# A graph layer on one core: the product of x made during the scatters and added by VectorE, and a written order for the last four node tiles

## The chip, the cores and the metric

The kernel runs on one core of a Trainium2 chip. A core has five engines with a queue of instructions each: TensorE (PE, whose weight loads the profile lists apart as PEld), VectorE (DVE), ScalarE (ACT), GpSimd (POOL) and SyncE (SP), and DMA engines that move data between memory and the core's two on-chip stores, SBUF and PSUM (where PE's products land). The engines run side by side and wait for each other by semaphores. The metric is the device time of one execution in microseconds (us).

## The reference

There are 6250 nodes with 128 features (x) and 206,250 edges with 128 features and a node number each (src). With the helper code left out, what is computed is

```python
def _L0_gnn_ref(x, edge_index, edge_features, global_feat, W_c, b_c, W1, b1, W2, b2, W3, b3):
    n = x.shape[0]
    row = edge_index[0]
    edge_aggr = jnp.zeros((n, HIDDEN), dtype=x.dtype).at[row].add(edge_features)
    global_expand = jnp.repeat(global_feat, n // global_feat.shape[0], axis=0)
    combined = jnp.concatenate([x, edge_aggr, global_expand], axis=-1) @ W_c + b_c
    h = jax.nn.softplus(combined @ W1 + b1)
    h = jax.nn.softplus(h @ W2 + b2)
    return h @ W3 + b3

edge_index = jnp.stack([src, dst])
x = _layernorm(x + _L0_gnn_ref(x, edge_index, edge_attr_128, ...), axis=-1)
```

The edges' rows are summed by node; then each node goes through a linear layer on (x, sum, global), two softplus layers, a last linear layer, the residual and a layer norm. All in float32.

## The kernel before, in words

**Sums by node.** The nodes are cut into buckets of 196 nodes (`BL`), and the kernel first brings the edges' rows into memory by bucket (`rows_by`), then sums each bucket with products of one-hot matrices. The edges are taken in columns of 122; two columns are a pair, three pairs a piece, and the pieces belong to eight groups (`GROUPS`). A piece passes through these steps:

- `load_rows`: SP loads 16 columns of edge rows (`rows`); `code_rows`: ACT writes their node numbers behind the features (`rows<-pair_i`, L1112).
- `compare`: a one-hot matrix of the rows' slots (`sort_hot`), by DVE (L1138) and ACT (L1145, L1147) in turn. `gather`: PE multiplies it with the rows (L1158) into one of three PSUM banks (`sorted`). `settle`: ACT copies the bank into one of six sets `pairs` (L1170).
- `scatter_row`: POOL sends a pair to its place in `rows_by` by an indirect DMA (L1187), 846 of them.
- position steps: for the groups ahead, short steps of PE and DVE find each edge's slot (`past` L723, `pair_ib` L494, products L553/L555/L738 into two PSUM banks that the profile calls `small`, `slot` L572).
- For each bucket, `chunks<-rows_by`: SP loads the sorted rows back; DVE makes the one-hot matrix `hot` (L986); PE sums (`part`, L1009); DVE adds the part to the columns of `sums_t` (L1030, L1032), which holds the sums turned (features on partitions, nodes in columns).

**What sets the order.** All of this is issued by hand. Each step is put on a list with a time of a plan in us (`when(t, step)`, `over(steps, t0, t1)` for several evenly apart), the list is sorted, and PE, DVE, ACT and SP issue in this order; POOL follows its own. In the plan a scatter takes 1.3 (`SCATTER`), and a piece's load, coding, compare, gather and settle are placed 36, 21, 17.5, 14 and 10.5 ahead of its first scatter. The profile's times lie near the plan's at first and some 20 us behind them in group 3. SP's queue is in order: a load that waits for its buffer holds all behind it.

**Weights.** `weights()`, planned at 100.0, loads the weights and `x_t`, x turned (128 partitions, 6250 columns; four DMAs). `combine` and `biases` of `node_rows()` work out the folded weights: `fold[:, 0]` = W_c's x part times W1, `fold[:, 1]` = its part for the sums times W1, and the biases; they run in group 3 (`NODES = (3, 4)`), from 477.9 us in the profile.

**The node layers** (`node_layers`, the tail). There are 13 tiles: eleven of 512 nodes, then 248 and 370. Their parts for the layer norm are tiles 0-2, 3-5, 6-8, then "two" (9 and 10, called a and b) and the end (11 and 12, c and d). The loop runs three tiles at once, one in each layer:

- `z_of(1)`: x's product and the sums' product go into one `sorted` bank (L1350, L1351). `decay` and `log1p`: ACT's Abs, Exp, Ln (L1361, L1362, L1367) from the bank to `away`. `softplus`: DVE makes `h` from the bank and `away` (L1375).
- `z_of(2)`: PE's product with W2 (L1354), then the same again. `last_product`: four products with W3 into a `small` bank (L1389).
- `last_layer`: DVE adds x (L1397) and takes mean and variance (L1400, L1404). `norm` (once for a part): DVE, ACT's two roots (L1415, L1416) and DVE again make 1/deviation (`rs`, L1414 to L1419); then y is scaled block by block, by POOL (L1431), in the two last parts every other block by ACT (L1428), at the very end by DVE instead of POOL; and stored.
- `summed_to`: PE's and DVE's sums of the last buckets (L1009, L1032) stand between these steps, as far as the next tile needs them.

The lines that set what `z_of` reads and where `norm` stands:

```python
                nc.tensor.matmul(z[:, :w], fold[:, 0, :], x_t[:, n0:n0 + w], start=True, stop=False)
                nc.tensor.matmul(z[:, :w], fold[:, 1, :], sums_t[:, n0:n0 + w],
                                 start=False, stop=True)
```

## Time and profile before

| what | us |
|---|---|
| median of three runs | 1322.09 (1319.48, 1322.09, 1325.66) |
| the profiled execution | 1324.44 |
| its span | 1322.7 |
| busy in the span: PE, DVE, ACT, POOL | 1170.2, 1073.0, 1064.5, 878.1 |
| POOL's scatters (846, L1187) | 825.7 busy, 329.9 idle before them |
| from 1188 to the end (the last buckets' sums and all node tiles) | 134.7 |

A row of the timeline is: start in us, duration, engine, line, operation, output and inputs with their sizes, xcount for several in a row; in brackets the idle time of the engine just before and what ended it ("DVE slot L572" is the operation on DVE of line 572 that wrote `slot`). A row of the waits is: who waited, for whom, the sum of the waits, how many, and the longest. In a row by line, the numbers behind a colon are the shortest, mean and longest duration in ns and the first and last start. Matmuls are shown by start and duration as a pipeline, so that two that follow each other may overlap.

### The profile page before, as it was taken

To read this page: it belongs to the slowest core of one execution; us is meant where nothing else is said; L and a number is where in the kernel's file an instruction comes from. 1 tells how busy PE (TensorE), PEld (TensorE's weight loads), DVE (VectorE), ACT (ScalarE), POOL (GpSimd) and SP (SyncE) were. 2 spreads that over 40 slices of the span, in tenths; PEclk is the share of its full clock that TensorE was granted. 3 is DMA by queue.
4 is the path that set the end of the run, shared out by engine and by line. 5 is a ranking of instruction groups with operands and counts; after the bars stand their busy time and mean duration, and the time that the engine had idled before them with its cause. 6 is when DMAs were issued, how large, how long until landed. Compare 5 with 4: busy or idle time off the path is not lost.

```text
span 1322.7 us, 26940 instructions
## 1 busy us (share of the span) xinstructions
PE 1170.2 (88%) x8617; PEld 1106.4 (84%) x8617; DVE 1073.0 (81%) x2403; ACT 1064.5 (80%) x2484; POOL 878.1 (66%) x915
## 2 busy tenths in 40 slices
...
GB/s 217 240 279 328 320 327 319 289 321 357 342 343 316 339 349 338 281 304 234 328 289 300 316 329 322 315 300 275 321 332 322 340 330 320 296 248 148 139 86 52
DMA packets 227251, 381.95 MB, mean 289 GB/s; under 512 B 28988, under 2 KB 140292, under 8 KB 226720
## 3 DMA queue, kind: packets, MB, share of 16 engines
...
q8 instruction: 72, 1.18, 0.4%
...
HBM read 237.21 MB, written 147.41 MB: 291 GB/s over the span
## 4 chain that ended last, share of the span: by engine, by line
PE 32%; DMA 28%; DVE 13%; ACT 9%; POOL 8%; issue 8%; SPq 1%; ACTq 0%; DVEq 0%; POOLq 0%
PE part L1009 19%; DMA chunks<-rows_by 11%; DMA rows_by<-pairs,pair 10%; PE sorted L1158 9%; POOL rows_by L1187 8%; DMA rows<-in_edge 6%; ACT pairs L1170 5%; DVE hot L986 3%; ACT sort_hot L1145 2%; DVE past L723 1%; DMA rows_by<-fill 1%; DVE sort_hot L1138 1%; DVE pair_ib L494 1%; DVE slot L572 1%; DVE sums_t L1032 1%
## 5 line engine op out<-in xcount | busy, mean ns | idle before, releaser
L1187 POOL DMA_INDIRECT rows_by<-pairs,pair x846 | 825.7, 976 | 329.9 <-issue 201.1
L1009 PE MATMUL part<-hot,chunks 128*128 128x196 f32 x3516 | 671.7, 334 | 16.9 <-DVE sums_t L1032 11.1
L1170 ACT COPY pairs<-sorted 64x387 f32<-64x387 f32 (+2 forms) x1144 | 542.6, 474 | 80.1 <-PE sorted L1158 60.1
L1009 PEld LDWEIGHTS part<-hot,chunks 128*128 128x128 f32 x3516 | 578.4, 192 | 26.2 <-DVE sums_t L1032 12.5
L1158 PE MATMUL sorted<-rows,sort_hot 122*128 122x129 f32 x3384 | 498.1, 287 | 58.7 <-ACT pairs L1170 49.5
L1158 PEld LDWEIGHTS sorted<-rows,sort_hot 122*128 122x128 f32 x3384 | 454.2, 198 | 72.4 <-ACT pairs L1170 69.6
L986 DVE TENSOR_TENSOR hot<-chunks,both_ps 128x784 f32<-128x784 f32 (+3 forms) x541 | 427.3, 808 | 19.2 <-DMA chunks<-rows_by 18.8
L1145 ACT ACTIVATE sort_hot<-plain,slot 122x128 f32<-122x128 f32 x846 | 278.3, 391 | 11.2 <-DVE slot L572 5.3
L1032 DVE TENSOR_TENSOR sums_t<-sums_t,part 128x392 f32<-128x392 f32 (+1 forms) x262 | 143.1, 546 | 133.7 <-PE part L1009 132.1
L1147 ACT ACTIVATE sort_hot<-sort_hot,ones 122x384 f32<-122x384 f32 (+2 forms) x286 | 174.6, 611 | 9.3
L1138 DVE TENSOR_TENSOR sort_hot<-slot,both_ps 122x384 f32<-122x384 f32 (+2 forms) x286 | 153.9, 539 | 3.2 <-PE sorted L1158 3.0
L494 DVE TENSOR_TENSOR pair_ib<-pair_block,both_ps 122x512 bf16<-122x512 bf16 (+2 forms) x157 | 103.2, 662 | 0.3
L1431 POOL TENSOR_SCALAR y<-y,mv,rs 128x128 f32<-128x128 f32 x40 | 31.1, 785 | 100.1 <-issue 70.8
L572 DVE TENSOR_REDUCE slot<-small 122x16 f32<-122x512 f32 (+2 forms) x109 | 72.6, 666 | 12.9 <-PE small L555 12.7
L1361 ACT ACTIVATE away<-sorted,z_bias 128x512 f32<-128x512 f32 (+2 forms) x13 | 8.5, 656 | 69.2 <-DMA chunks<-rows_by 44.6
L553 PE MATMUL small<-pair_ib,half 122*122 122x512 bf16 (+2 forms) x109 | 43.0, 395 | 14.1 <-DVE slot L572 13.8
L1112 ACT COPY rows<-pair_i 122x16 f32<-122x16 f32 x106 | 22.6, 213 | 37.5 <-DMA rows<-in_edge 36.6
L738 PEld LDWEIGHTS <-past 128*128 128x128 f16 x424 | 24.7, 98 | 20.3 <-DVE past L723 14.7
L738 PE MATMUL small<-jump,past 128*128 128x56 f16 (+3 forms) x424 | 29.1, 189 | 13.5 <-DVE past L723 8.9
L723 DVE TENSOR_TENSOR past<-both_ps,starts 128x512 f16<-128x512 f32 (+1 forms) x61 | 39.7, 663 | 0.2
L555 PEld LDWEIGHTS <-starts_h 128*122 128x122 bf16 x236 | 25.3, 148 | 16.3 <-issue 11.9
L723 DVE TENSOR_TENSOR past<-both_ps,starts_late 128x512 f16<-128x512 f32 (+2 forms) x49 | 32.2, 659 | 0.0
...
## 6 DMA issues: line engine op xcount, KB each, us to landing
...
rows_by<-pairs,pair POOLq DMA_INDIRECT x846
...
```

Source lines behind the costliest of these rows:

```text
L494: nc.vector.tensor_tensor(ib, pair_block[:, cols].unsqueeze(2).to_broadcast([PN, n, SB]), iota_ps[:PN, :SB].unsqueeze(1).to_broadcast([PN, ...
L572: nc.vector.tensor_reduce(to, of, axis=mybir.AxisListType.X, op=ALU.max)
L723: nc.vector.tensor_tensor(past[:, :, a:b], twice_ps[:KB].unsqueeze(1).unsqueeze(1).to_broadcast([KB, 2, b - a, P // 2]), own["starts"][:, ...
L986: nc.vector.tensor_tensor(hot[:, q - a:q - a + m], chunks[j][:, lo:hi + 1:step, D:W].to_broadcast([P, m, BL]), iota_ps.unsqueeze(1).to_bro ...
L1009: nc.tensor.matmul(part[:, b - base_of[v], :], t[:, place_in(j, q), :D], hot[:, q - a], start=first, stop=last)
L1032: nc.vector.tensor_add(here, here, of)
L1138: nc.vector.tensor_tensor(hot[:PN, :m], slot[:PN, at:at + 2 * m - 1:2].unsqueeze(2).to_broadcast([PN, m, P]), slot_ps[:PN].unsqueeze(1).to ...
L1145: nc.scalar.activation(hot[:PN, j], by_slot[:PN], AF.Abs, bias=slot[:PN, at:at + 1], scale=-1.0)
L1147: nc.scalar.activation(hot[:PN, :m], hot[:PN, :m], AF.Relu, bias=ones[:PN, :1], scale=-1.0)
L1158: nc.tensor.matmul(out[:, j, :], hot[:PN, j], rows_at[col // LOAD_COLS][:PN, col % LOAD_COLS, :], start=True, stop=True)
L1170: nc.scalar.copy(sets_at[i][64 * n:64 * n + 64, lo:lo + m, h, :W], out[64 * h:64 * h + 64, :m, :])
L1187: s = nc.gpsimd.indirect_dma_start(out=dst, out_offset=bass.IndirectOffsetOnAxis(ap=at, axis=0), in_=rows[:, j].rearrange("p a b -> p (a b ...
```

## The change

- `weights()` is planned at 60.0 instead of 100.0.
- `combine` and `biases` are planned at 130 and 141 instead of in group 3; `NODES` goes.
- 13 new steps `times` (every 13 from 150): PE multiplies 512 columns of `x_t` with `fold[:, 0]` into a `small` bank; 3.5 of plan later `kept` copies the bank by ACT over the same columns of `x_t`. From then on `x_t` holds the product.
- In the tail `z_of(1)` makes the sums' product alone; `with_x` on DVE adds `x_t` to it into a new SBUF tile `z_x` (three buffers), which ACT and the softplus of layer 1 read in the bank's place. It stands behind the first three steps of `summed_to`, ahead of the remaining ones.
- `norm` is split into `roots` (DVE's first step and ACT's two) and the rest.
- The loop ends four steps earlier, and the layers of tiles a, b, c, d stand in an order written out.

```diff
@@ -64,11 +64,12 @@
 FIRST = 24.0
 SOON, FLAGGED = 4.0, 15.9
 SHARE = 2
+KEPT = 3.5
 PREP, LAG = 0.85, 11.0
 TOGETHER, BEHIND = 2, 1
-AT_END, FIRST_STEPS = 4, 9
+AT_END, FIRST_STEPS, X_STEPS = 4, 9, 3
 MATCHED, MULTIPLIED, RATE = 9.0, 1.5, 0.58
-NODES = (3, 4)
+FOLDED, TIMES, EVERY = 130.0, 150.0, 13.0
 TURNED = 2048
 APART = 3
 BATCH = 4
@@ -1092,7 +1093,16 @@
                 nc.tensor.matmul(small[:, 0, :], b2_all, w_sb["w3"], start=True, stop=True)
                 nc.vector.tensor_add(b3_all, small[:, 0, :], of_weights["b3"])
 
-            return [combine, biases]
+            of = {}
+
+            def times(a, b):
+                of[a] = small_bank().rearrange("p b n -> p (b n)")[:, :b - a]
+                nc.tensor.matmul(of[a], fold[:, 0, :], x_t[:, a:b], start=True, stop=True)
+
+            def kept(a, b):
+                nc.scalar.activation(x_t[:, a:b], of.pop(a), AF.Copy)
+
+            return combine, biases, times, kept
 
         pieces = [(g, t, min(PAIRS, s1 - t)) for g, (s0, s1) in enumerate(groups)
                   for t in range(s0, s1, PAIRS)]
@@ -1275,7 +1285,14 @@
             positions_0 = positions(0)[0]
             over([lambda: node_codes(0), tables] + positions_0[:12] + [more_tables] + positions_0[12:], -8.0, FIRST - 19.0)
             when(FLAGGED, lambda: flags_0[0]())
-            when(100.0, weights)
+            when(60.0, weights)
+            combine, biases, times, kept = node_rows()
+            when(FOLDED, combine)
+            when(FOLDED + LAG, biases)
+            for k, a in enumerate(range(0, N, 4 * P)):
+                t, b = TIMES + k * EVERY, min(N, a + 4 * P)
+                when(t, lambda a=a, b=b: times(a, b))
+                when(t + KEPT, lambda a=a, b=b: kept(a, b))
 
             def fills_left():
                 assert not fills
@@ -1290,7 +1307,6 @@
 
             when(begins[last_pair], count_over)
             when(ends[-1], lambda: fills_left())
-            nodes, held = node_rows(), 0
             ahead_of = {g: [(g + 1, 0)] for g in range(G - 1)}
             ahead_of[GAP - 1] = [(GAP, 1)]
             for k in range(GAP, G):
@@ -1308,15 +1324,7 @@
                         prep += [lambda k=k: node_codes(k)]
                         position_steps[k] = positions(k)
                     prep += position_steps[k][part]
-                if NODES[0] <= g < NODES[1]:
-                    upto = len(nodes)
-                    part = nodes[held:upto]
-                    held = upto
-                    middle = t0 + PREP * (t1 - t0)
-                    over(part, middle, t1)
-                    over(prep, t0, middle)
-                else:
-                    over(prep, t0 if g else 16.0, t0 + PREP * (t1 - t0))
+                over(prep, t0 if g else 16.0, t0 + PREP * (t1 - t0))
             todo = fill_rows()
             done_by = FIRST + SCATTER * todo[-1][0] - SLACK
             for n, (due, _, step) in enumerate(todo):
@@ -1347,12 +1355,15 @@
         def z_of(layer, n0, w):
             z = bank()
             if layer == 1:
-                nc.tensor.matmul(z[:, :w], fold[:, 0, :], x_t[:, n0:n0 + w], start=True, stop=False)
-                nc.tensor.matmul(z[:, :w], fold[:, 1, :], sums_t[:, n0:n0 + w],
-                                 start=False, stop=True)
+                nc.tensor.matmul(z[:, :w], fold[:, 1, :], sums_t[:, n0:n0 + w], start=True, stop=True)
             else:
                 nc.tensor.matmul(z[:, :w], w_sb["w2"], h1.pop(n0)[:, :w], start=True, stop=True)
             sub_z[layer, n0] = [z]
+
+        def with_x(n0, w):
+            z = work.tile([P, 4 * P], F32, name="z_x", bufs=3)
+            nc.vector.tensor_add(z[:, :w], sub_z[1, n0][0][:, :w], x_t[:, n0:n0 + w])
+            sub_z[1, n0] = [z]
 
         def decay(layer, n0, w):
 
@@ -1365,6 +1376,10 @@
         def log1p(layer, n0, w):
             away = sub_z[layer, n0][1]
             nc.scalar.activation(away[:, :w], away[:, :w], AF.Ln, bias=ones[:, :1])
+
+        def away_of(layer, n0, w):
+            decay(layer, n0, w)
+            log1p(layer, n0, w)
 
         def softplus(layer, n0, w):
 
@@ -1405,19 +1420,22 @@
             now["done"].append((n0, w, y, at))
             now["at"] += -(-w // P)
 
-        def norm(now, late, last):
-
+        def roots(now, late, last):
             mv, nb = now["mv"], now["at"]
             rs = work.tile([P, 3, 16], F32, name="rs", bufs=2)
             v, g, t = (rs[:, k, :nb] for k in range(3))
-            minus = work.tile([P, 16], F32, name="minus", bufs=2)[:, :nb]
+            now["roots"] = v, g, t
             nc.vector.tensor_scalar(v, mv[:, :nb, 1], EPS, None, op0=ALU.add)
             nc.scalar.activation(t, v, AF.Ln)
             nc.scalar.activation(g, t, AF.Exp, scale=-0.5)
+
+        def norm(now, late, last):
+            mv, nb, (v, g, t) = now["mv"], now["at"], now["roots"]
             nc.vector.tensor_mul(t, g, g)
             nc.vector.scalar_tensor_tensor(t, t, -0.5, v, op0=ALU.mult, op1=ALU.mult)
             nc.vector.scalar_tensor_tensor(g, t, 1.5, g, op0=ALU.add, op1=ALU.mult)
             if late:
+                minus = work.tile([P, 16], F32, name="minus", bufs=2)[:, :nb]
                 nc.vector.scalar_tensor_tensor(minus, mv[:, :nb, 0], -1.0, g,
                                                op0=ALU.mult, op1=ALU.mult)
             for n0, w, y, at in now["done"]:
@@ -1453,11 +1471,13 @@
             summed_to(0)
             z_of(1, *tiles[0])
             normed = None
-            for step in range(len(tiles) + 2):
-                first, second, third = (tiles[k] if 0 <= k < len(tiles) else None
-                                        for k in (step, step - 1, step - 2))
+            for step in range(len(tiles) - 2):
+                first, second, third = (tiles[k] if k >= 0 else None for k in (step, step - 1, step - 2))
+                summed_to(step + 1, X_STEPS)
+                if first:
+                    with_x(*first)
                 if step + 1 < len(tiles):
-                    summed_to(step + 1, FIRST_STEPS)
+                    summed_to(step + 1, FIRST_STEPS - X_STEPS)
                 if second:
                     z_of(2, *second)
                 if third:
@@ -1467,21 +1487,55 @@
                     last_product(*third)
                 for layer, tile_ in ((1, first), (2, second)):
                     if tile_:
-                        decay(layer, *tile_)
-                        log1p(layer, *tile_)
+                        away_of(layer, *tile_)
                 if third:
                     last_layer(now, *third)
                     if third == parts[k][-1]:
-                        normed = (now, k >= len(parts) - 2, k == len(parts) - 1)
-                if step + 1 < len(tiles):
-                    summed_to(step + 1)
-                    z_of(1, *tiles[step + 1])
+                        normed = (now, False, False)
+                summed_to(step + 1)
+                z_of(1, *tiles[step + 1])
                 for layer, tile_ in ((1, first), (2, second)):
                     if tile_:
                         softplus(layer, *tile_)
-                if normed:
+                if normed and step < len(tiles) - 3:
+                    roots(*normed)
                     norm(*normed)
                     normed = None
+
+            a, b, c, d = tiles[-4:]
+            assert [list(part) for part in parts[-2:]] == [[a, b], [c, d]] and normed
+            two, end = (open_part(part) for part in parts[-2:])
+            with_x(*c)
+            summed_to(len(tiles) - 1)
+            z_of(2, *b)
+            last_product(*a)
+            z_of(1, *d)
+            away_of(1, *c)
+            away_of(2, *b)
+            roots(*normed)
+            last_layer(two, *a)
+            norm(*normed)
+            softplus(1, *c)
+            softplus(2, *b)
+            z_of(2, *c)
+            last_product(*b)
+            with_x(*d)
+            away_of(1, *d)
+            away_of(2, *c)
+            softplus(1, *d)
+            z_of(2, *d)
+            last_layer(two, *b)
+            softplus(2, *c)
+            away_of(2, *d)
+            last_product(*c)
+            softplus(2, *d)
+            roots(two, True, False)
+            last_layer(end, *c)
+            norm(two, True, False)
+            last_product(*d)
+            last_layer(end, *d)
+            roots(end, True, True)
+            norm(end, True, True)
 
     node_layers(rest, lambda: summed["to"])
     slow = ctx.enter_context(tc.tile_pool(name="slow", bufs=1))
```

How the instructions stand now (names with `rows`, `fill`, `chunks` as above; `h_...` with `neg_z` is layer 1, with `neg_b` layer 2).

SP's queue, around the loads of the weights and `x_t`, before:

```order
L291 DMA rows<-in_edge 10x4x516
L291 DMA chunks<-rows_by 128x2x136 x6
L291 DMA rows_by<-fill 128x4x272
L291 DMA weights_sb<-in_weights 128x900
L291 DMA x_t<-in_x_turned 128x2048 x3
L291 DMA x_t<-in_x_turned 128x106
L291 DMA rows<-in_edge 112x4x516
L291 DMA rows<-in_edge 10x4x516
L291 DMA chunks<-rows_by 128x2x136 x2
```

And now:

```order
L292 DMA rows<-in_edge 10x4x516
L292 DMA rows_by<-fill 128x4x272
L292 DMA weights_sb<-in_weights 128x900
L292 DMA x_t<-in_x_turned 128x2048 x3
L292 DMA x_t<-in_x_turned 128x106
L292 DMA rows<-in_edge 112x4x516
L292 DMA rows<-in_edge 10x4x516
L292 DMA rows_by<-fill 128x4x272
```

The five loads stand four rows loads, four fills and the first six chunk loads earlier, and no longer just ahead of the two chunk loads.

ACT's queue among the scatters, where the first copy stands now (nothing stood there before):

```order
L1180 COPY pairs_108<-sorted 64x3x129 x4
L1103 ACTIVATE x_t<-small 128x512
L1155 ACTIVATE sort_hot<-plain,slot 122x128 x3
L1157 ACTIVATE sort_hot<-sort_hot,ones 122x384
L1180 COPY pairs_109<-sorted 64x3x129 x4
```

The copy waits for PE's product of the same columns, and the settles and compares of the pieces behind it wait in ACT's queue.

DVE's queue in the last tiles, from the softplus of a in layer 1 to that of c, before:

```order
L1375 SCALAR_TENSOR_TENSOR h_14977<-sorted,neg_z,away 128x512
L1375 SCALAR_TENSOR_TENSOR h_14979<-sorted,neg_b_75,away 128x512
L1414 TENSOR_SCALAR rs<-mv 128x12
L1417 TENSOR_TENSOR rs<-rs 128x12
L1418 SCALAR_TENSOR_TENSOR rs<-rs 128x12
L1419 SCALAR_TENSOR_TENSOR rs<-rs 128x12
L1032 TENSOR_TENSOR sums_t<-sums_t,part 128x392
L1397 TENSOR_TENSOR y<-small,x_sb 128x512
L1400 BN_STATS stats<-y 128x6 x4
L1404 BN_AGGR mv<-stats 128x2 x4
L1375 SCALAR_TENSOR_TENSOR h_15040<-sorted,neg_z,away 128x248
```

And now:

```order
L1390 SCALAR_TENSOR_TENSOR h_15026<-sorted,neg_b_75,away 128x512
L1365 TENSOR_TENSOR z_x<-sorted,x_t 128x248
L1033 TENSOR_TENSOR sums_t<-sums_t,part 128x392
L1428 TENSOR_SCALAR rs<-mv 128x12
L1412 TENSOR_TENSOR y<-small,x_sb 128x512
L1415 BN_STATS stats<-y 128x6 x4
L1419 BN_AGGR mv<-stats 128x2 x4
L1434 TENSOR_TENSOR rs<-rs 128x12
L1435 SCALAR_TENSOR_TENSOR rs<-rs 128x12
L1436 SCALAR_TENSOR_TENSOR rs<-rs 128x12
L1390 SCALAR_TENSOR_TENSOR h_15089<-z_x,neg_z,away 128x248
```

The three `rs` steps for which POOL waits with y of tiles 6 to 8 stood ahead of y of tile a, and stand behind it and its statistics now; `z_x` and the add of the last buckets come in between.

ACT's queue at the same place, before:

```order
L1367 ACTIVATE away<-away,ones 128x512
L1415 ACTIVATE rs<-rs 128x12
L1416 ACTIVATE rs<-rs 128x12
L1361 ACTIVATE away<-sorted,z_bias 128x248
L1362 ACTIVATE away<-away 128x248
L1367 ACTIVATE away<-away,ones 128x248
L1361 ACTIVATE away<-sorted,b_c 128x512
```

And now:

```order
L1372 ACTIVATE away<-z_x,z_bias 128x248
L1373 ACTIVATE away<-away 128x248
L1378 ACTIVATE away<-away,ones 128x248
L1372 ACTIVATE away<-sorted,b_c 128x512
L1373 ACTIVATE away<-away 128x512
L1378 ACTIVATE away<-away,ones 128x512
L1429 ACTIVATE rs<-rs 128x12
L1430 ACTIVATE rs<-rs 128x12
L1372 ACTIVATE away<-z_x,z_bias 128x370
```

The two roots of tiles 6 to 8 passed behind the layer 1 of c and the layer 2 of b.

## The prediction

> **What bounds the kernel now.** I read the page first (engines, chain, groups), then the stretches by window, then the waits of the two places that the change touches, and last the end in order of time.
>
> ```profile
> span 1322.7 us, 26940 instructions
> PE 1170.2 (88%) x8617; PEld 1106.4 (84%) x8617; DVE 1073.0 (81%) x2403; ACT 1064.5 (80%) x2484; POOL 878.1 (66%) x915
> PE 32%; DMA 28%; DVE 13%; ACT 9%; POOL 8%; issue 8%; SPq 1%; ACTq 0%; DVEq 0%; POOLq 0%
> L1187 POOL DMA_INDIRECT rows_by<-pairs,pair x846 | 825.7, 976 | 329.9 <-issue 201.1
> ```
>
> No engine has the chain to itself. Windows give the stretch and its length, the busy time of PE, PE's weight loads, DVE, ACT and POOL with their instructions, then the granted clock, the DMA share and GB/s:
>
> ```profile
> 55.00:65.00 10.00, 7.79 (x77) 6.69 (x74) 9.59 (x27) 8.97 (x24) 7.23 (x8) 0.97 0.55 157
> 132.00:198.00 66.00, 56.97 (x470) 53.27 (x469) 59.46 (x130) 63.23 (x149) 50.04 (x52) 0.97 1.02 324
> 462.00:528.00 66.00, 55.95 (x412) 54.44 (x411) 51.20 (x122) 57.11 (x138) 46.46 (x48) 0.95 1.04 344
> 660.00:858.00 198.00, 196.90 (x1457) 194.30 (x1458) 160.71 (x310) 183.28 (x435) 149.72 (x155) 0.98 0.99 311
> 1188.00:1284.00 96.00, 88.88 (x452) 72.58 (x451) 76.21 (x171) 37.32 (x58) 22.17 (x30) 1.00 0.45 132
> ```
>
> The limit changes by stage. From 132 to 198 POOL issues 52 scatters in 66 us, one per 1.27 us: POOL's own pace bounds, with ACT (63.2 of 66) close behind and DMA full. From 660 PE is busy 196.9 of 198 us. In the tail (from 1188: the node layers) it is PE with DVE, and at the end a chain through every engine. So an edit is worth something only where it meets the limit of its own stage. The rows between loads, scatters and their waits (SP's queue, then the engines):
>
> ```profile
> 46.51 0.39 SPq L291 DMA_DIRECT2D rows_by<-fill  x1
> 60.59 0.79 SPq L291 DMA_DIRECT2D rows<-in_edge  x2
> 97.42 2.45 SPq L291 DMA_DIRECT2D x_t<-in_x_turned  x4
> 106.96 2.38 SPq L291 DMA_DIRECT2D chunks<-rows_by  x2
> 122.94 0.56 DVE L986 TENSOR_TENSOR hot<-chunks,both_ps 128x392 f32<-128x392 f32 x1 [4.51 <-DMA chunks<-rows_by]
> 125.90 0.59 PE L553 MATMUL small<-pair_ib,half 122*122 122x512 bf16 x1 [6.26 <-DVE slot L572]
> 132.13 0.97 POOL L1187 DMA_INDIRECT rows_by<-pairs,pair  x1 [6.46 <-ACT pairs L1170]
> 133.40 0.97 POOL L1187 DMA_INDIRECT rows_by<-pairs,pair  x1 [0.30 <-issue]
> 392.20 0.97 POOL L1187 DMA_INDIRECT rows_by<-pairs,pair  x1 [1.02 <-ACT pairs L1170]
> ```
>
> **Term A, the loads moved up: -6.2.** The four x_t loads and the weights leave their place behind a rows load and in front of the chunks' load, and stand behind the fill of 46.51. The chunk load issued at 106.96 landed 16 us later; DVE waited 4.51 for it, PE 6.26 for DVE, and POOL's scatter 6.46 through ACT. POOL then goes back to its pace, 0.97 of work and 0.30 of issue: a stall of 6.16 at POOL in a stretch that POOL bounds, so its end moves the whole plan. In the new place the DMA share is 0.55, and the rows load now behind it (60.59) is what could be late: its coding on ACT ran only at 82.45, 20 us after.
>
> ```profile
> 82.45 0.22 ACT L1112 COPY rows<-pair_i 122x16 f32<-122x16 f32 x1
> ACT pairs L1170 <- PE sorted L1158: 6.0, 6, 1.8
> 1287.39 0.69 ACT L1361 ACTIVATE away<-sorted,z_bias 128x512 f32<-128x512 f32 x1 [0.51 <-PE sorted L1351]
> ```
>
> I take 6.2 off; the ends are 6.5 off and nothing (the chunk load is late for another reason). On SP's queue the five loads pass four rows loads, four fills and six chunk loads; SP has nothing to issue from 46.9 to 60.59, and the x_t issue takes 2.45. POOL's queue is not passed.
>
> **Term B, 13 products and 13 copies among the scatters: +1.0.** PE gets 13 matmuls of 128x512 (1.02 for a pair of halves, row in term D), 13 us in 156 us of plan, and has 9 us idle in the window of 66, so nothing at PE. ACT gets 13 copies, PSUM to SBUF. No row is such a copy; nearest is another ACT function from PSUM, 128x512, 0.69 (L1361, third row above): 12 x 0.69 + 0.2 = 8.5 us. What hides it: ACT's 6.0 us of waits for PE (second row above: sum, count, longest; from 132 to 330) and the lead of its plan, since POOL waits for ACT at 132.13 and then not before 392.20. 8.5 against 6.0 leaves 2.5; the lead of the plan takes some, so +1.0, between 0 and 8.5 (all of it on POOL's pace, the lead gone).
>
> **Term C, folding the weights at plan 130 instead of 478: 0.** The same instructions in another place. At 462 to 528 they lay where POOL does 48 scatters and is itself held up; the first of them was short:
>
> ```profile
> L1075 PE MATMUL small<-weights_sb x4: 275/275/356, 477.9 to 478.3; 128*128 128x128 f32 x4
> ```
>
> What hides them at 130 is the two "small" banks and PE's idle time; if that is gone, the chain of some ten short steps holds DVE's position steps for 3 us. Bounds -1 and +3.
>
> **Term D, x's products gone from the tail: -4.3.** 13 accumulating pairs become single products.
>
> ```profile
> L1350 PE MATMUL sorted<-x_t,fold x26: 373/592/595, 1191.6 to 1295.2; 128*128 128x512 f32 x22, 128*128 128x248 f32 x2, 128*128 128x370 f32 x2
> 1199.28 1.02 PE L1350 MATMUL sorted<-x_t,fold 128*128 128x512 f32 x2
> 1200.13 1.02 PE L1351 MATMUL sorted<-sums_t,fold 128*128 128x512 f32 x2
> 1240.49 1.12 PE L1351 MATMUL sorted<-sums_t,fold 128*128 128x512 f32 x2 [1.18 <-DVE sums_t L1032]
> 1257.90 1.02 PE L1350 MATMUL sorted<-x_t,fold 128*128 128x512 f32 x2
> DVE y L1397 <- PE small L1389: 15.5, 9, 2.6
> PEld sorted L1351 <- DVE sums_t L1032: 6.6, 6, 2.0
> ```
>
> From 1199.28 to 1200.13 x's half costs PE 0.85 or 0.86. At 1240.49 the sums half waits for DVE's add all the same: there x's half only fills the wait. By that reading the removal gains in the pairs at 1199.28, 1206.49, 1230.17, 1251.12 and 1257.90, which stand without a wait (first and last of the five quoted), and nothing in the four that wait (1219.58, 1240.49, 1268.81, 1279.44), in the first, released by an add that had just ended, or in the last three, which belong to term F: 5 x 0.86 = 4.3. Bounds: 13 x 0.86 = 11.2, and nothing.
>
> **Term E, DVE's 13 new adds: +1.3.** An add of DVE, then two places where PE waits for one:
>
> ```profile
> 1285.67 0.69 DVE L1397 TENSOR_TENSOR y<-small,x_sb 128x512 f32<-128x512 f32 x1 [1.85 <-PE small L1389]
> 1245.29 1.59 PE L1009 MATMUL part<-hot,chunks 128*128 128x196 f32 x8 [1.02 <-DVE sums_t L1032]
> 1273.14 1.59 PE L1009 MATMUL part<-hot,chunks 128*128 128x196 f32 x8 [1.21 <-DVE sums_t L1032]
> ```
>
> Nearest is y at L1397, PSUM plus SBUF, 128x512, 0.69, of which some 0.65 is its share in a queue. By count that is 13 x 0.65 = 8.5 (two tiles are narrower), the upper bound. DVE waited 15.5 us for PE in the same stretch (nine times, y at L1397 in the rows above), which hides most. On the path are the two places where PE's products waited for an add that a new add now stands ahead of: 2 x 0.65 = 1.3.
>
> **Term F, the end's own order: +5.2.** In order of time, DVE, ACT, POOL:
>
> ```profile
> 1288.76 0.55 DVE L1032 TENSOR_TENSOR sums_t<-sums_t,part 128x392 f32<-128x392 f32 x1
> 1293.81 0.21 ACT L1415 ACTIVATE rs<-rs 128x12 f32<-128x12 f32 x1 [2.13 <-DVE rs L1414]
> 1294.71 0.17 DVE L1419 SCALAR_TENSOR_TENSOR rs<-rs 128x12 f32<-128x12 f32 x1
> 1294.99 3.89 POOL L1431 TENSOR_SCALAR y<-y,mv,rs 128x128 f32<-128x128 f32 x5 [12.19 <-DVE rs L1419]
> 1303.19 0.29 DVE L1417 TENSOR_TENSOR rs<-rs 128x8 f32<-128x8 f32 x1 [0.57 <-ACT rs L1416]
> 1306.49 3.11 POOL L1431 TENSOR_SCALAR y<-y,mv,rs 128x128 f32<-128x128 f32 x4
> 1313.58 1.26 ACT L1428 ACTIVATE y<-y,minus,rs 128x128 f32<-128x128 f32 x3 [0.83 <-DVE minus L1421]
> L1603 POOLq DRAIN  x3: 40/113/9306, 1312.5 to 1322.4; - x3
> ```
>
> POOL starts on y of tiles 6 to 8 when DVE has rs (1294.99), works without a gap to 1309.60, and its queue ends with a drain of 9.3 us, from 1312.5 to 1321.8: the last thing in the span. ACT's last y ends at 1314.84. I take the drain to follow POOL's last y at a fixed distance. In the new order the first product of tile 10 gets its x on DVE behind the add of 1288.76: 1289.31 + 0.65 = 1289.95, where ACT read the bank at 1287.39, so ACT is 2.6 later; with steps of 2.1 (three functions, 0.69 at the row of 1287.39 and the two behind it) ACT does away of 10, then of 9, to 1294.2; y of 9 and z_x of 11 follow on DVE to 1295.3, away of 11 (1.5) and of 10 (2.1) on ACT to 1298.95, now ahead of the roots, two roots 0.45, three rs on DVE 0.65: POOL starts at about 1300.15, 5.2 later than 1294.99. The wait that goes is ACT's 2.13 for rs; late next is POOL, behind it its 12 scalings, three stores and four scalings. The path of ACT and DVE, where away of tile 12 now passes the scalings of y, ends at 1315.35 by the same steps against 1314.84: +0.5. Bounds: +5.2, and -2 (the two ends decoupled, and the hand order saves what ACT waited for rs).
>
> **Term G, the shared port: +0.3.** The row at 1303.19, a DVE operation from SBUF alone beside POOL's y, took 0.29, its like before (1294.71, another rs step, POOL idle) 0.17. Four of the softplus operations now read SBUF alone and fall beside POOL's y; four times 0.12 is about 0.5, of which 0.3 is on the path. The Trainium skill ("SBUF — State Buffer", section "Who interferes with whom") says that a VectorE instruction with both inputs in SBUF is locked out for the whole of a GpSimd instruction that reads SBUF, and one with an input in PSUM is not: this speaks against the change. At POOL's 3.89 / 5 = 0.78 a y that rule would make it up to 3.1 and the sum 2.8 worse; the row at 1303.19 shows less.
>
> **Sum.** -6.2 + 1.0 + 0 - 4.3 + 1.3 + 5.2 + 0.3 = -2.7. The profiled execution took 1324.44 (span 1322.7, 1.7 around it), the median 1322.09, so 0.9982 of it: (1324.44 - 2.7) x 0.9982 = 1319.4. Half a per cent, 6.6 us, is about what a measurement of this kernel tells from no change.
>
> **Rivals.** R1, faster: the drain has its own length and the end follows ACT and DVE, so that POOL's delay is hidden. Then F is +0.5: -7.4, 1314.7. For it: ACT's last y (1314.84) ends 5 us after POOL's last, and the store of it is still to come. Against: the drain ends the span and starts 2.9 after POOL's last y.
>
> R2, slower, one mechanism: ACT becomes the bound at plan 150 to 306. Each copy stands in ACT's order 3.5 us of plan behind its product; where PE is late, ACT waits inside the copy with all its settles behind it. At half the longest wait for PE, 1.8 (quoted), that is 13 x (0.65 + 0.9) = 20, less 8 of cover: 12 for term B instead of 1.0, sum +8.3, 1330. It decides (+0.5% in all) from 9.3 more than I gave, 0.7 a copy. For it: ACT is busy 63.2 of 66. Against: POOL does not wait for ACT there in any row.
>
> R3: the move of the loads does not do what it seems to. The chunk load of 106.96 is late by the full DMA share of its time, or POOL's earlier plan is given back from 392, where POOL waits for ACT again (1.02) with the DMA share full (1.04 from 462): term A is 0, sum +3.5, 1325.6.
>
> **How the numbers follow.** The forecast has 0.37, R1 0.29, R2 0.18, R3 0.16. The likeliest is 1319.4, alone from 1315 to 1324. A gain beyond R1 is open through D (to 11.2). The range leaves out R2's upper half and D's far end: 1311 to 1329. Faster by over 0.5% (under 1315.5): R1's larger half and the forecast's lower edge, 0.34. Slower by over 0.5% (above 1328.7): most of R2 and the edge of R3, 0.19. The rest, 0.47.
>
> **What would show it.** A: no wait of over 2 us at POOL near 132, and the scatter then at that place some 6 us earlier; wrong if a rows load's coding is waited for near 82. B: the copies at 0.6 to 0.7 each and POOL still at 52 scatters per 66 us; wrong (R2) if POOL shows waits for ACT between 150 and 330. D and E: 13 single pairs of halves at L1351's place, PE's busy time in the tail 11 us less, its waits for sums a little longer; wrong if the tail shortens by 8 or more. F: POOL's y starting only behind DVE's y of tile 9 and its statistics, and the drain again 2.9 after POOL's last y; if the drain starts or ends otherwise, R1. Together they are wrong if the stretch from 392 to 860 gives back or adds more than these 6 us, since I left its plan as it is.

## The result, and the profile after

The changed kernel takes 1335.32 us in the median of 15 runs (1326.37 to 1344.02), the kernel before 1322.70 in 15 runs beside it (1318.08 to 1337.33). The ratio on record is 1.0064, with a 95% interval of 1.0042 to 1.0085: some 8.5 us slower (5.6 to 11.2), where 2.7 us faster was forecast. It is not the quotient of the medians, which lie 12.6 us apart (the means 10.3); the ratios below are not the quotients of the medians beside them either. The profiled execution of the changed kernel is the slowest of its 15, 1344.02 us, so its trace loses more than the kernel does as a rule. Four of the five groups of runs below met chips on which the kernel before takes 1600 to 1628 us (mean granted clock of TensorE 0.895 to 0.912 in the profiled executions, POOL waiting for ACT every few scatters) instead of the 1328 us of the fifth group (0.955 to 0.964).

The page of the changed kernel, the same lines as before:

```profile
span 1342.2 us, 26955 instructions
PE 1185.9 (88%) x8617; PEld 1119.9 (83%) x8617; DVE 1080.1 (80%) x2416; ACT 1071.2 (80%) x2497; POOL 879.1 (66%) x915
PE 41%; DMA 26%; DVE 15%; ACT 7%; issue 5%; POOL 4%; SPq 1%; ACTq 0%; DVEq 0%; POOLq 0%
L1197 POOL DMA_INDIRECT rows_by<-pairs,pair x846 | 825.6, 976 | 343.0 <-issue 205.6
```

POOL's scatters are busy for the same time to 0.1 us, the idle time ahead of them is 13 us longer. PE has taken 9 points of the chain, POOL has lost 4: the scatters now wait longer.

Where the time goes is told best by the starts of single scatters, counted from 0 in the two traces:

| scatter | before | after | difference |
|---|---|---|---|
| 60 | 101.65 | 101.63 | -0.02 |
| 90 | 146.19 | 140.60 | -5.59 |
| 120 | 185.04 | 183.69 | -1.34 |
| 180 | 262.09 | 263.84 | +1.75 |
| 270 | 377.42 | 381.20 | +3.77 |
| 420 | 594.75 | 598.55 | +3.80 |
| 600 | 831.90 | 835.78 | +3.88 |
| 660 | 911.32 | 922.28 | +10.96 |
| 845 (the last) | 1155.76 | 1168.79 | +13.03 |

The stall at 132 is gone as forecast, and 9.4 us are lost between scatters 90 and 270. The rows of POOL's queue where the loss begins:

```profile
156.01 0.97 POOL L1197 DMA_INDIRECT rows_by<-pairs,pair  x1 [2.23 <-ACT pairs L1180]
161.68 0.97 POOL L1197 DMA_INDIRECT rows_by<-pairs,pair  x1 [2.14 <-ACT pairs L1180]
```

And of ACT's, two settles ahead of them and the first copy:

```profile
145.19 0.97 ACT L1180 COPY pairs<-sorted 64x387 f32<-64x387 f32 x2 [1.57 <-PE sorted L1168]
154.77 0.97 ACT L1180 COPY pairs<-sorted 64x387 f32<-64x387 f32 x2 [2.21 <-PE sorted L1168]
165.08 0.60 ACT L1103 ACTIVATE x_t<-small 128x512 f32<-128x512 f32 x1
```

ACT's wait for PE from 132 to 330 in the view of the waits:

```profile
ACT pairs L1180 <- PE sorted L1168: 11.0, 10, 2.7
```

And all copies, in the view of the tile `x_t`:

```profile
L1103 ACT ACTIVATE x_t<-small x13: 260/597/597, 165.1 to 324.1; 128x512 f32<-128x512 f32 x12, 128x106 f32<-128x106 f32 x1
```

The first stalls come ahead of the first copy (165.08). ACT waits for PE, 11.0 us where it had waited 6.0: the copies, 0.60 each, are not the first thing to look at. The window in which POOL did 52 scatters before:

```profile
132.00:198.00 66.00, 57.83 (x442) 53.79 (x442) 53.82 (x123) 57.48 (x137) 46.37 (x48) 0.95 0.93 301
```

48 scatters, and only PE is busy more of the time than before, by 0.9 us; ACT is busy 57.5 against 63.2 of 66. So it is not ACT's work that got too much, but its waiting.

The last 9.2 us, between scatters 600 and 845, are of another kind. From 660 to 1150 us ACT waits for the loads of edge rows. The waits of before, of the changed kernel and of t1_roots_first, a run below with the same main phase:

```profile
ACT rows L1112 <- DMA rows<-in_edge: 19.3, 10, 6.4
ACT rows L1122 <- DMA rows<-in_edge: 29.6, 16, 4.0
ACT rows L1122 <- DMA rows<-in_edge: 14.6, 12, 4.2
```

Where ACT waits 10.3 longer than before, 9.2 us are lost from scatter 600 to 845; where it waits 4.7 less, 2.3 are won. The change has no step of its own in this stretch (its last copy starts at 324.1), and the same main phase gave more in one execution and less in the other. So I do not count these 9 us as the change's. What made the loads late in that execution is not shown.

In the tail I measure from the first product of the sums of tile 0 to the end. Before, that is from 1192.45 to 1322.67, 130.2 us; after, from 1207.26 to 1342.16, 134.9. The rows of the end, PE's first, then POOL's, DVE's and ACT's:

```profile
1207.26 1.02 PE L1358 MATMUL sorted<-sums_t,fold 128*128 128x512 f32 x2
1313.00 4.42 POOL L1449 TENSOR_SCALAR y<-y,mv,rs 128x128 f32<-128x128 f32 x5 [17.38 <-DVE rs L1436]
1325.67 3.11 POOL L1449 TENSOR_SCALAR y<-y,mv,rs 128x128 f32<-128x128 f32 x4 [0.70 <-DVE rs L1436]
1324.10 0.18 DVE L1419 BATCH_NORM_AGGREGATE mv<-stats 128x2 f32<-128x6 f32 x1 [2.58 <-POOL y L1449]
1329.41 1.26 ACT L1446 ACTIVATE y<-y,minus,rs 128x128 f32<-128x128 f32 x3 [0.83 <-DVE minus L1439]
```

The drain, in the view by line:

```profile
L1657 POOLq DRAIN  x3: 40/113/9306, 1332.0 to 1341.9; - x3
```

POOL's last y ends at 1328.78, its drain again takes 9.306 us and starts 3.2 behind it (before 2.9). The last 0.8 us are common to both kernels. So the tail's 4.7 us stand in POOL's queue, as the forecast had it.

### The profile page after: what moved, and what is told of

Same layout as the page of the kernel before. It is cut to its first block, busy times and chain, and to the rows that moved or that the text cites. A ratio compares the mean times of both kernels' runs of the same rounds, so it can differ in the third digit from the quotient of the medians.

```text
span 1342.2 us, 26955 instructions
## 1 busy us (share of the span) xinstructions
PE 1185.9 (88%) x8617; PEld 1119.9 (83%) x8617; DVE 1080.1 (80%) x2416; ACT 1071.2 (80%) x2497; POOL 879.1 (66%) x915
## 3 DMA queue, kind: packets, MB, share of 16 engines
q8 instruction: 72, 1.18, 0.4%
## 4 chain that ended last, share of the span: by engine, by line
PE 41%; DMA 26%; DVE 15%; ACT 7%; issue 5%; POOL 4%; SPq 1%; ACTq 0%; DVEq 0%; POOLq 0%
PE part L1010 23%; DMA chunks<-rows_by 13%; PE sorted L1168 12%; DMA rows<-in_edge 9%; ACT pairs L1180 4%; DVE hot L987 4%; POOL rows_by L1197 3%; DMA rows_by<-pairs,pair 3%; ACT sort_hot L1155 2%; DVE past L724 1%; DVE sort_hot L1148 1%; SPq L292 1%; DVE sums_t L1033 1%; DVE pair_ib L495 1%; PE small L554 1%
## 5 line engine op out<-in xcount | busy, mean ns | idle before, releaser
L1010 PE MATMUL part<-hot,chunks 128*128 128x196 f32 x3516 | 681.8, 338 | 13.3 <-DVE sums_t L1033 8.4
L1010 PEld LDWEIGHTS part<-hot,chunks 128*128 128x128 f32 x3516 | 588.3, 194 | 23.3 <-DVE sums_t L1033 9.8
L1168 PEld LDWEIGHTS sorted<-rows,sort_hot 122*128 122x128 f32 x3384 | 458.8, 199 | 79.0 <-ACT pairs L1180 75.6
L1449 POOL TENSOR_SCALAR y<-y,mv,rs 128x128 f32<-128x128 f32 x40 | 32.3, 815 | 105.1 <-issue 70.1
L1372 ACT ACTIVATE away<-z_x,z_bias 128x512 f32<-128x512 f32 (+2 forms) x13 | 9.0, 696 | 90.8 <-DVE z_x L1365 45.7
L739 PEld LDWEIGHTS <-past 128*128 128x128 f16 x424 | 25.0, 99 | 18.8 <-DVE past L724 12.6
```

The source lines that it names most:

```text
L1010: nc.tensor.matmul(part[:, b - base_of[v], :], t[:, place_in(j, q), :D], hot[:, q - a], start=first, stop=last)
L1168: nc.tensor.matmul(out[:, j, :], hot[:PN, j], rows_at[col // LOAD_COLS][:PN, col % LOAD_COLS, :], start=True, stop=True)
```

## The experiments

On the chips of 1600 us nothing of the main phase's single stalls can be read (the traces of s1_main_only and s2_after, one main phase on one chip, lie 5.0 us apart at scatter 270); the tail is the same to 0.1 us on all of them, and its distances can be compared across. The tail's table (us from tile 0's first sums product):

| kernel | tile 8's product | POOL starts on tiles 6 to 8 | POOL's last y ends | last y of ACT or DVE ends | end |
|---|---|---|---|---|---|
| before | 76.4 | 102.5 | 117.2 | 122.4 | 130.2 |
| changed | 74.2 | 105.7 | 121.5 | 123.4 | 134.9 |
| e4_tail_only | 74.2 | 105.7 | 121.5 | 123.4 | 134.9 |
| t2_no_x | 74.0 | 100.4 | 115.0 | 120.3 | 128.1 |
| t3_order_only | 76.4 | 105.1 | 120.4 | 122.3 | 133.8 |
| t1_roots_first | 74.2 | 103.0 | 118.9 | 120.8 | 132.3 |
| b1_loads_dve | 76.4 | 102.6 | 113.3 | 122.4 | 129.5 |
| b2_end | 76.4 | 102.6 | 112.0 | 122.1 | 128.2 |

And the main phase on the chip of 1328 us, as differences of a scatter's start from the trace of the kernel before (another run; m2, m3 and t1 are 0.7 to 1.2 later at scatter 60 already, which is taken off in what follows). Each column is one execution; those of m3 and t1 are the fastest of their ten:

| scatter | m1_loads | m2_fold | m3_no_copies | t1_roots_first (main phase of the change) | changed |
|---|---|---|---|---|---|
| 60 | -0.15 | +0.68 | +0.92 | +1.18 | -0.02 |
| 90 | -6.09 | -4.35 | -4.36 | -3.89 | -5.59 |
| 120 | -6.45 | -1.96 | -1.72 | -1.47 | -1.34 |
| 180 | -4.52 | -1.73 | +1.69 | +2.01 | +1.75 |
| 270 | -3.42 | -0.58 | +2.38 | +4.13 | +3.77 |
| 480 | -3.73 | -0.11 | -0.10 | +2.87 | +3.82 |
| 600 | -2.32 | +0.95 | -0.75 | +2.67 | +3.88 |
| 845 | +1.93 | +3.13 | -0.87 | +0.35 | +13.03 |

At the last scatter the columns stand in no order that fits the edits (m3_no_copies is ahead of m1_loads). What single scatters show of the change, they show up to about scatter 480; behind it the waits for the loads of edge rows cover it.

### The parts of the main phase

The loads alone, e1_loads_early and, as m1_loads, once more:

```diff
-            when(100.0, weights)
+            when(60.0, weights)
```

> The kernel before with one edit: the loads of the weights and of x_t planned at 60 instead of 100. Theory 1 (ACT's pace comes from the copies): POOL's stall at 132 goes and nothing is given back, so scatter 270 comes 5.5 us earlier than before (377.4) and the time is 4 to 6 us less. Rival (the stall was ACT's lead: settles and scatters run at the same pace, and without the 6 us pause ACT's late settles show as stalls from 146 on): scatter 270 at 376 to 378, time unchanged within 2 us.

Measured with the kernel before at 1628.03: 1631.88 (1.0021, 0.9986 to 1.0055). With POOL stalling throughout, the expected scatter could not be looked for.

> The kernel before with the loads of the weights and of x_t planned at 60 instead of 100, once more, for conditions under which the kernel before takes some 1322 us. Theory 1 (what is lost again after 132 is lost to the folding, the products and the copies): POOL's stall at 132 goes, nothing is given back, scatter 270 comes at 372 (before 377.4) and the time is 4 to 6 us less. Rival (the pause at 132 was where ACT got its lead over POOL; without it ACT's own pace shows as stalls): scatter 270 at 375 to 378, time within 2 us of before.

Measured: 1326.60 against 1327.98 (0.9988, 0.9954 to 1.0022). Scatter 120 comes 6.45 us earlier, so the stall of 132 was the loads'. Between scatters 150 and 270 three of the 6.4 are given back (scatter 270 at 374.0: between the two theories), and by the time nothing is to be told from no change.

The loads and the folding, e2_fold_early and m2_fold:

```diff
-            when(100.0, weights)
+            when(60.0, weights)
+            combine, biases = node_rows()
+            when(130.0, combine)
+            when(130.0 + LAG, biases)
...
-            nodes, held = node_rows(), 0
+            nodes, held = [], 0
```

> As e1_loads_early, and the folding of the weights and the biases planned at 130 and 141, with no product of x and no copy. Theory 1: like e1 at every scatter to within 1 us. Rival (the folding makes the stalls of 156.0 and 161.7, which come before the first copy at 165.1 in the changed kernel): scatter 120 some 4 us later than in e1, and the time 4 us over e1's.

Measured: 1632.43 against 1628.03 (1.0031, 1.0000 to 1.0063), where the stalls could not be told apart.

> As m1_loads, and the folding of the weights and the biases planned at 130 and 141; no product of x, no copy. Theory 1 with the copies as its main part: scatter 120 within 1 us of m1_loads. Rival (the folding makes the stalls of 156.0 and 161.7, which come ahead of the first copy at 165.1): scatter 120 some 4 us later than in m1_loads, and POOL stalls near 156 and 162.

Measured: 1329.77 against 1327.98 (1.0011, 0.9984 to 1.0038), and the rival holds in the main. Scatter 120 comes 4.5 later than in m1_loads, 3.7 of it behind scatter 60. Of the 3.7, 0.9 are lost by scatter 90, with a wait of POOL's of 1.18 at 127.75, ahead of the folding's first product (136.46). From 120 to 126 the granted clock (third number from the end) was another, m1_loads first, then m2_fold:

```profile
120.00:126.00 6.00, 3.63 (x28) 3.00 (x27) 6.00 (x21) 3.67 (x10) 4.50 (x5) 1.00 0.50 131
120.00:126.00 6.00, 5.31 (x23) 4.92 (x23) 5.93 (x25) 2.67 (x7) 4.54 (x5) 0.51 0.51 173
```

PE's same eight sums (L1009) took 1.90 and 2.92 us in it. In m3_no_copies, t1_roots_first and the changed kernel the clock there was 0.52, 0.50 and 0.72, and 0.7, 0.9 and 0.4 were lost by scatter 90. Whether the edits bring the clock down or chance does is not shown. The folding's own steps are left with 2.7 us between scatters 90 and 120 (3.0 and 2.8 in m3 and t1, 4.6 in the changed kernel's trace). The rows of m2_fold, PE first, then POOL:

```profile
152.47 0.28 PE L1081 MATMUL small<-c_bias,weights_sb 128*128 128x1 f32 x2
153.54 0.38 PE L1086 MATMUL small<-z_bias,weights_sb 128*128 128x1 f32 x2 [0.79 <-DVE z_bias L1082]
154.60 0.49 PE L1092 MATMUL small<-weights_sb,b_all 128*128 128x128 f32 x2 [0.68 <-DVE b_all L1090]
157.04 0.97 POOL L1187 DMA_INDIRECT rows_by<-pairs,pair  x1 [2.54 <-ACT pairs L1170]
```

ACT's whole wait for PE from 132 to 165 in m2_fold:

```profile
ACT pairs L1170 <- PE sorted L1158: 3.8, 3, 2.5
```

And the same in m1_loads, which has no folding there:

```profile
ACT pairs L1170 <- PE sorted L1158: 0.9, 1, 0.9
```

Each product of the biases needs DVE's result of the one ahead, and PE's queue is in order: PE stands 0.79 and 0.68 us, the next gathers come behind 154.93, ACT's settle waits 2.5 and POOL 2.54 (2.24 over its pace).

The change without its copies, m3_no_copies:

```diff
                 when(t, lambda a=a, b=b: times(a, b))
-                when(t + KEPT, lambda a=a, b=b: kept(a, b))
```

> The changed kernel without ACT's 13 copies (the products of x are made and dropped; the node layers add x itself, so x's term of the output is left unmultiplied). If the copies take ACT's time from the settles: from scatter 120 to 270 no loss against before (192 us; the changed kernel 197.5), and the time 5 us under the changed kernel's. If PE's products or the folding are what costs: 197 us there, and the changed kernel's time.

Measured: 1335.03 against 1327.98 (1.0057, 1.0026 to 1.0087). From scatter 120 to 270 it takes 196.5 us, m2_fold 193.8, the changed kernel 197.5. So neither expectation in full: of the loss against m2_fold at scatter 270, the products alone make 2.7 (2.96, less 0.25 at scatter 60), and the copies 1.5 more by the trace of t1_roots_first, 2.3 by that of the changed kernel. At scatter 480 the split is another: without the copies nothing is lost against m2_fold (-0.10 against -0.11), with them 2.5 in t1_roots_first. And by the time, leaving the copies out brought nothing: 1335.03 here, 1333.22 in t1_roots_first, whose end comes 2.6 earlier. Together products and copies cost 4.2 to 5.1 at scatter 270; which of the two it is stays open.

The change's main phase with the tail of before, s1_main_only, u1_main_only and first e3_main_only (the functions of the node layers are those of before):

```diff
-                nc.tensor.matmul(z[:, :w], fold[:, 1, :], sums_t[:, n0:n0 + w], start=True, stop=True)
+                nc.tensor.matmul(z[:, :w], fold[:, 0, :], x_t[:, n0:n0 + w], start=True, stop=False)
+                nc.tensor.matmul(z[:, :w], fold[:, 1, :], sums_t[:, n0:n0 + w],
+                                 start=False, stop=True)
...
```

> The changed kernel up to the last scatter with the node layers of the kernel before (x_t then holds the product, which is multiplied once more: x's term in the output is a wrong one, the work is that of the tail before). Theory 1: scatter 270 at 381, 3.8 us later than before, and from the last scatter to the end 167 us as before: time 4 to 6 us over the kernel before. Rival (most of the loss is the tail's): time within 2 us of before or less.

> The changed kernel up to the last scatter with the node layers of the kernel before (x's product is multiplied once more; x's term of the output is a wrong one, the work is the tail's of before), for conditions under which the kernel before takes some 1322 us. From the first product of tile 0 to the end 130.2 as before. If the part of the main phase in the loss is what the scatters show at scatter 600 (3.9): time 3 to 5 us over before. If the 13 us that the profiled execution had lost by the last scatter are the change's: 9 to 13 us over before.

> As s1_main_only, for conditions under which the kernel before takes some 1322 us: scatter 270 some 4 us later than before; 1.002 to 1.004 of before if the loss at scatter 600 is all of the main phase's, 1.007 or more if the 13 us of the profiled execution are the change's.

Measured: 1630.83 against 1628.03 (1.0018, 0.9986 to 1.0050), 1605.85 against 1603.56 (1.0031, 0.9999 to 1.0062) and 1604.11 against 1601.10 (1.0010, 0.9984 to 1.0035), all three where the kernel before takes 1600 or more. By these ratios the main phase's part there is 2 to 5 us, though no change lies inside each interval; the tail's distances are those of before. The 9 to 13 us of the second expectation are not seen, but these chips are not the ones it was meant for.

The changed kernel beside them, s2_after and u2_after (no edit):

> The changed kernel once more beside the others. If main phase and tail add up: s1_main_only's loss and 4.7 us, 1.006 to 1.007 of before.

> The changed kernel beside it: u1_main_only's ratio and 4.7 us (0.0035).

Measured: 1605.28 against 1603.56 (1.0031, 1.0005 to 1.0057) and 1609.48 against 1601.10 (1.0035, 1.0003 to 1.0068). On these chips the loss is 5 to 6 us. The sum that was expected of s2_after (1.006 to 1.007) lies outside its interval: its ratio is that of s1_main_only, though its tail takes 4.7 us longer in the trace. Parts of 2 to 5 us cannot be told apart by such times; the tail's part is shown by the traces.

The products later, m4_products_later:

```diff
-FOLDED, TIMES, EVERY = 130.0, 150.0, 13.0
+FOLDED, TIMES, EVERY = 465.0, 500.0, 9.0
```

> The changed kernel with folding, products and copies later: folding at plan 465 and 476 (about its place before), the 13 products every 9 from 500 on, where ACT is busy 51 to 57 of 66 us and POOL waits in any case. If folding and products cost because they stand where POOL runs at its own pace without a lead: scatter 270 at 372 to 375 as in m1_loads, at most 2 us lost between scatters 330 and 480 against m1_loads, and the time 3 to 5 us under the changed kernel's. If they cost wherever they stand: 4 to 7 us lost in that stretch, time as the changed kernel's.

Measured: 1618.04 against 1600.77 (1.0087, 1.0057 to 1.0118), the largest ratio of all runs, though its interval overlaps that of the changed kernel. From scatter 390 to 450, where the products now stand, it takes 110.1 us; b1_loads_dve, t3_order_only and t2_no_x, without products there, take 103.1, 101.4 and 99.7 on the same chip. Later was not cheaper. Since POOL waits throughout there, what the later place would cost at 1322 us is not shown.

### The parts of the tail

The changed tail alone, e4_tail_only (the main phase and `x_t` of before):

```diff
-                nc.tensor.matmul(z[:, :w], fold[:, 0, :], x_t[:, n0:n0 + w], start=True, stop=False)
-                nc.tensor.matmul(z[:, :w], fold[:, 1, :], sums_t[:, n0:n0 + w],
-                                 start=False, stop=True)
+                nc.tensor.matmul(z[:, :w], fold[:, 1, :], sums_t[:, n0:n0 + w], start=True, stop=True)
...
+                    with_x(*first)
...
```

> The kernel before up to the last scatter with the changed kernel's node layers (x itself, not its product, is added, so x's term in the output is left unmultiplied). If the tail alone loses what the traces show (166.9 us from the last scatter to the end before, 173.4 after): 6 us over before. By the forecast's terms D, E, F and G it would be 2.5 over. By the rival that the order written out hides POOL's delay it would be 2 under.

Measured: 1630.17 against 1628.03 (1.0031, 1.0004 to 1.0057), and in the trace every distance of the changed tail: 4.7 us to the end. The 166.9 and 173.4 of the expectation also hold 36.7 and 38.5 from the last scatter to tile 0's product, a distance that lies between 35 and 43 in the runs with either tail.

Without x's product, t2_no_x:

```diff
-                nc.tensor.matmul(z[:, :w], fold[:, 0, :], x_t[:, n0:n0 + w], start=True, stop=False)
-                nc.tensor.matmul(z[:, :w], fold[:, 1, :], sums_t[:, n0:n0 + w],
-                                 start=False, stop=True)
+                nc.tensor.matmul(z[:, :w], fold[:, 1, :], sums_t[:, n0:n0 + w],
+                                 start=True, stop=True)
```

> The kernel before without x's 26 matmuls in the node layers, and nothing in their place (x's term is left out of layer 1). This is term D alone. From the first product of tile 0 to that of tile 8 the kernel before takes 76.4 us, the changed one 74.2; to the end 130.2 and 134.9. By term D: 72.1 to tile 8 (five pairs of 0.86 less), the end at 126. If PE is not what bounds the tail: 75.5 to 76.4, the end at 129.5 or more.

Measured: 1595.28 against 1600.77 (0.9963, 0.9926 to 1.0000). Tile 8's product comes at 74.0, the end at 128.1: 26 products less bring 2.4 and 2.1 us, half of term D. Next to it the changed loop (74.2) shows that the eight adds up to tile 8's product cost 0.2.

The written order alone, t3_order_only (the change's tail without `with_x`, x's product in layer 1):

```diff
-                nc.tensor.matmul(z[:, :w], fold[:, 1, :], sums_t[:, n0:n0 + w], start=True, stop=True)
+                nc.tensor.matmul(z[:, :w], fold[:, 0, :], x_t[:, n0:n0 + w], start=True, stop=False)
+                nc.tensor.matmul(z[:, :w], fold[:, 1, :], sums_t[:, n0:n0 + w],
+                                 start=False, stop=True)
...
-                if first:
-                    with_x(*first)
...
-            with_x(*c)
...
-            with_x(*d)
```

> The kernel before with the written order of the last four tiles alone: x's product stays in layer 1, no add of x. This is term F without the add. Up to tile 8 as before (76.4). If the later roots are what delays POOL: its first y of tiles 6 to 8 at 105 to 107.5 (before 102.5), its last at 120 to 122 (117.2), the end 133 to 135. If the delay comes from the add of x standing in the chain instead: 102.5 to 103.5, and the end within 1 of before's 130.2.

Measured: 1604.64 against 1600.77 (1.0032, 0.9997 to 1.0067). POOL starts at 105.1 and the end comes at 133.8: 3.6 us from the order alone.

The roots of tiles 6 to 8 back in their old place, t1_roots_first:

```diff
+            roots(*normed)
+            norm(*normed)
             away_of(1, *c)
             away_of(2, *b)
-            roots(*normed)
             last_layer(two, *a)
-            norm(*normed)
```

> The changed kernel with the roots and the norm of tiles 6 to 8 back ahead of layer 1 of tile 11 and layer 2 of tile 10. From the first product of tile 0 to POOL's last y the kernel before takes 117.2 us, the changed one 121.5; to the end 130.2 and 134.9. If the end follows POOL's last y (drain 9.3 us, some 3 behind it): POOL starts on tiles 6 to 8 some 5 us earlier, its last y at 116 to 117, the end at 129.5 to 130.5. If the drain has its own length or ACT and DVE are the bound: POOL's y earlier by as much, the end still at 134 or more.

Measured: 1333.22 against 1327.98 (1.0053, 1.0027 to 1.0079). POOL starts 2.7 earlier than in the changed kernel, not 5, its last y ends 2.6 earlier, and the end comes 2.6 earlier (132.3). The end follows POOL's y; half of POOL's delay, 2.7 of 5.4 behind tile 8's product, was not the roots' place. POOL's rows in this run:

```profile
1294.47 4.18 POOL L1449 TENSOR_SCALAR y<-y,mv,rs 128x128 f32<-128x128 f32 x5 [14.63 <-DVE rs L1436]
1307.28 3.12 POOL L1449 TENSOR_SCALAR y<-y,mv,rs 128x128 f32<-128x128 f32 x4 [1.06 <-DVE rs L1436]
```

And its drain:

```profile
L1657 POOLq DRAIN  x3: 40/113/9306, 1313.6 to 1323.5; - x3
```

### A better end

POOL's last four scalings given to DVE, with the loads at 60, b1_loads_dve:

```diff
-                        (nc.vector if last else nc.gpsimd).tensor_scalar(
+                        (nc.vector if late else nc.gpsimd).tensor_scalar(
...
-            when(100.0, weights)
+            when(60.0, weights)
```

> The kernel before with the loads planned at 60, and with the four scalings of y of tiles 9 and 10 that POOL did done by DVE. If the end follows POOL's last y: it comes 3.3 us earlier, the end at 127 to 128 behind tile 0's first product (before 130.2, where the path of ACT, DVE and the last store takes over), and the time 3 to 6 us under the kernel before. If the drain does not follow POOL: the end at 130.2 to 131.4.

Measured: 1601.86 against 1600.77 (0.9997, 0.9967 to 1.0027). POOL's last y ends 3.9 earlier, the end comes 0.7 earlier. The drain now begins 5.7 behind POOL's last y, no longer 2.9: what POOL did last is the store of tile 8. So the stores were moved too, b2_end and u3_end:

```diff
-                    (sync_dma if late else nc.gpsimd.dma_start)(
+                    (sync_dma if late or n0 >= tiles[-7][0] else nc.gpsimd.dma_start)(
```

> The kernel before with the loads planned at 60, the four scalings of y of tiles 9 and 10 by DVE instead of POOL (as b1_loads_dve), and the three stores of tiles 6 to 8 issued by SP instead of POOL. If the drain follows POOL's last store as well as its last y: the end 127 to 128 behind tile 0's first product (b1_loads_dve 129.5, before 130.2), the time 3 to 6 us under before. If it was POOL's y alone that held it, or the last store on SP: 129 or more.

> As b2_end, whose end came at 128.2 instead of 130.2 with the time not to be told from before. By the scatters of m1_loads and this end: 2 to 5 us under before, 0.996 to 0.9985. If the loads' gain is given back whole by the last scatter: 0.9985 to 1.0.

Measured: 1598.97 against 1603.56 (0.9995, 0.9965 to 1.0024) and 1601.09 against 1601.10 (1.0001, 0.9969 to 1.0033). The end comes at 128.2, 2.0 before that of the kernel before, and not at 127; the 3 to 6 us by which the time was to be shorter are not seen, nor the 2 to 5 of u3_end. The rows of b2_end:

```profile
L1603 POOLq DRAIN  x3: 40/113/9061, 1581.3 to 1594.5; - x3
L1603 SPq DRAIN  x3: 7/7/13, 1593.9 to 1594.2; - x3
```

POOL's long drain is over at 1590.4 (1581.35 and 9.06), and the end waits for SP's at 1593.9, behind the last store: by these rows the bound is now ACT, DVE and that store. The 2 us are real in the trace and too few for the time to show where runs differ by 1%. No version was shown to beat the kernel before.

## Why the prediction was wrong

The forecast of -2.7 lay outside what came, and 1335.32 above the range. By its own terms:

- **A, the loads: right in its place, not in its worth.** m1_loads shows 6.45 us at scatter 120, -6.2 was forecast. But 3 of them are gone by scatter 270, all of them at the last scatter of its trace, and the time of m1_loads cannot be told from no change. I had taken the stall to move the whole plan; R3 had named the giving back, from 392 on, and it began near 220.
- **C, the folding: the step that failed first.** Forecast 0, bounds -1 and +3; measured 2.7 to 3.0 between scatters 90 and 120 in the three runs of one chip, 4.6 in the changed kernel's trace. Against m1_loads m2_fold is 2.0 behind at scatter 270 and 2.8 at 480. I took PE's 9 us of idle time in the window for cover. The chain of products and DVE steps does not need idle time somewhere; it holds PE's queue in one place, where the gathers that POOL waits for stand behind it. What it had cost in group 3, where POOL was held up anyway, no run measured alone.
- **B, products and copies: mis-sized.** Forecast +1.0, with the copies as the cost and the products at nothing. Measured 4.2 to 5.1 for both at scatter 270, within the bound of 8.5; their split (2.7 for the products there, nothing at scatter 480) is not settled, so that taking the products for nothing is not shown to be the fault. A copy takes 0.60, not 0.69. The mechanism of R2 was named, but with ACT as the bound: ACT's busy time fell, its waits for PE rose from 6.0 to 11.0.
- **A to C together:** 3.8 us lost by scatter 270 and the same at scatter 600 in the changed kernel's trace, 2.9 and 1.5 in that of t1_roots_first, where -5.2 was forecast. This is the larger half of the miss.
- **D, x's products: half.** Forecast -4.3, measured -2.4 up to tile 8 and -2.1 at the end. Pairs without a wait were counted as gain; part of it went into longer waits for DVE's adds behind them (the rows below; at the place of the last one the wait before was 0.1).

PE's waits at the sums products, before and after, and its row at tile 9 in the changed kernel:

```profile
PE sorted L1351 <- DVE sums_t L1032: 2.6, 3, 1.2
PE sorted L1358 <- DVE sums_t L1033: 6.4, 5, 2.0
1292.68 1.12 PE L1358 MATMUL sorted<-sums_t,fold 128*128 128x512 f32 x2 [0.96 <-DVE sums_t L1033]
```

- **E, the adds: smaller in the loop, larger at the end.** Forecast 1.3; 0.2 up to tile 8. At the end, order and adds together put POOL's start 31.5 us behind tile 8's product (105.7 - 74.2) where it was 26.1: 5.4, of which the order alone makes 2.6 (t3_order_only, 28.7). The other 2.8 came with the adds in place of x's products; the products' going alone makes 0.3 (t2_no_x, 26.4).
- **F, the end's order: right.** Forecast 5.2 later for POOL's start, with the add in the chain; measured 5.4 from tile 8's product. The drain follows POOL: R1 falls. POOL's chain then is 15.8 us long and not 14.7, which the forecast did not have, and the drain begins 0.3 later behind it: -2.2 up to tile 8, 5.4, 1.1 and 0.3 make 4.6 of the 4.7.
- **G, the shared port: right in kind.** Layer 1's softplus beside POOL's y took 0.92 where it had taken 0.74 (tile 5 in both kernels). Before:

```profile
1251.45 0.74 DVE L1375 SCALAR_TENSOR_TENSOR h<-sorted,neg_z,away 128x512 f32<-128x512 f32 x1
```

And after, with the softplus of layer 2 behind it, and POOL's three y beside both (before 2.34):

```profile
1264.38 0.92 DVE L1390 SCALAR_TENSOR_TENSOR h<-z_x,neg_z,away 128x512 f32<-128x512 f32 x1
1265.22 0.74 DVE L1390 SCALAR_TENSOR_TENSOR h<-sorted,neg_b,away 128x512 f32<-128x512 f32 x1
1263.73 2.85 POOL L1449 TENSOR_SCALAR y<-y,mv,rs 128x128 f32<-128x128 f32 x3
```

The one that reads SBUF alone is slower, the one that reads a bank behind it is not. The Trainium skill ("SBUF — State Buffer", section "Who interferes with whom") makes the shared port pair an exclusive lock, for which a VectorE instruction with two SBUF inputs contends with a GpSimd instruction that reads SBUF. The traces agree that the two contend, on both sides; less than a whole instruction is lost, since each met what was left of the other. The softplus met a y of POOL's with 0.14 us left and took 0.18 longer; POOL's next y met the softplus with 0.79 left and took 1.29 instead of 0.78, 0.51 longer. And a small step loses little or nothing: the one behind the row at 1303.19, also from SBUF alone and inside the same y of POOL's, took 0.17, which is what it takes with POOL idle. At the end the loss is POOL's: its first five y of tiles 6 to 8 take 4.42 in the changed kernel, 3.89 before, and 3.90 in t3_order_only, which has the order but no operand z_x. That is 0.5 on the path, where 0.3 was forecast, and half of the 1.1 by which POOL's chain is longer.

The tail's terms D to G made +2.5 in the forecast and 4.7 in the traces, the same in all six traces with this tail. Of the ratio's 8.5 us that leaves 3.8 for the main phase, of the interval's ends 0.9 and 6.5. That the changed kernel's trace also shows 3.8 at scatter 600 is chance: the same main phase shows 1.5 there in t1_roots_first. How much of what the main phase loses by scatter 480 reaches the end is not shown by any single trace.
